# Layer 1's cross-attention as a pipeline of single tiles, three of them begun in the self-attention

## The chip, the cores and the metric

The kernel runs on one core of a Trainium2 chip. A core has a matrix engine (TensorE, PE in the profile, with its weight loads as PEld), three engines for elementwise work (VectorE or DVE, ScalarE or ACT, GpSimd or POOL), and queues that start transfers (SyncE, or SP). Every engine works through its own instructions in order, and engines wait for each other through semaphores. TensorE writes to PSUM, which holds eight banks of 128 x 512 floats; the other memory is SBUF.

The metric is the device time of one execution in microseconds. A lower number is better.

## The reference

Two decoder layers with a layernorm after each sub-layer work on `x` of shape (2, 1024, 256), so on 2048 tokens. The change lies in the second layer's cross-attention, and it reaches into the self-attention before it:

```python
def _L1_xattn_ref(q, k, v, mask, wq, wk, wv, wo):
    # q: x (2, 1024, 256); k and v: ctx_1024 (2, 64, 256); 16 heads of 16
    qh = (q @ wq.T).reshape(bs, sq, N_HEADS, D_K).transpose(0, 2, 1, 3)
    kh = (k @ wk.T).reshape(bs, sk, N_HEADS, D_K).transpose(0, 2, 1, 3)
    vh = (v @ wv.T).reshape(bs, sk, N_HEADS, D_K).transpose(0, 2, 1, 3)
    z = jnp.einsum('bhqd,bhkd->bhqk', qh, kh) / math.sqrt(D_K)
    z = jnp.where(mask[:, None, :, :], jnp.float32(-10000000000.0), z)
    z = jax.nn.softmax(z, axis=-1)
    z = jnp.einsum('bhqk,bhkd->bhqd', z, vh)
    z = z.transpose(0, 2, 1, 3).reshape(bs, sq, D_MODEL)
    return z @ wo.T

x = _layernorm(x + _L1_attn_ref(...))     # x + 16-head self-attention, 1024 x 1024 scores
x = _layernorm(x + _L1_xattn_ref(x, ctx_1024, ctx_1024, mask_BxSxS2_bk1, wq, wk, wv, wo))
x = _layernorm(x + _L1_ffn_ref(x, ...))   # quantised: needs the largest |x| of all tokens first
```

Each token has 16 heads x 64 keys = 1024 scores. The feed-forward network after it scales its input by the largest absolute value of the whole layernorm's output, so it cannot begin before the last tile has been normalised.

## The kernel before

The 2048 tokens are four groups of 512 (`g`), two for each batch element, and 16 tiles of 128 (`n`). The stages follow each other: layer 0's attention, cross-attention and experts (`l0_attn`, `l0_xattn`, `l0_ffn`), layer 1's self-attention (`l1_attn`, L1205), its cross-attention (`l1_xattn`, L1647) and its feed-forward network (`l1_ffn`). While the experts run, the generator `prepare` (L1518) makes ready what layer 1 will need, one step of it at each of the expert steps from the fifth on: here the masks, the transposed weights of the cross-attention, its keys (`lxkT`) and values (`vblk`), and the quantised weights of the last network.

Inside a `manual_schedule` the engines that it names issue in the order in which the program is written. The other engines' order is made by a planner.

The self-attention goes by units. A unit is one block of 128 keys for four heads and 512 queries; there are 16 steps of 8 units. In each unit `maxima` computes scores on TensorE and takes their maxima on VectorE nine units ahead (L1285, L1295), `products` computes the scores again, transposed (L1331), adds the shift (L1338) and takes the exponentials on ScalarE (L1348), and `mix` multiplies those of the unit before by the values (L1362). Every eighth unit `shifts` and `shifted` turn the maxima into the next step's shift (GpSimd L1307 to L1309, TensorE L1316). The table `extra` puts other work behind the unit's own: `taken` and `quotient` for the step before (L1382 to L1387), and after the last heads of a group `turned` (L1400), `residual` (L1410, GpSimd), `output` (L1418), `normed` and `onward` (L154). What is left for the last group after the last unit is in `self.ends`, which the cross-attention calls. The written order holds for TensorE, VectorE and ScalarE there; GpSimd's is the planner's.

In the cross-attention only TensorE's order is written. A tile passes through these steps:

- `queries(g)` for a group: 2 x 2 products of 512 columns (L1671), scaled by 0.25 on the way out.
- `softmax(n)`: GpSimd fills a tile with -1e10 (L1683); TensorE computes the 1024 scores in two products over 128 rows, against keys laid out block by block so that each head meets only its own 16 rows (`kblk`, L1686); VectorE copies the scores that are not masked over the fill (L1690) and takes each head's maximum (L1695); GpSimd subtracts it (L1696); ScalarE takes the exponential (L1697).
- `turn(n)`: 8 transposes (L1707), copied out of PSUM by ScalarE and VectorE.
- `mix(n)`: 8 products of 34 columns (L1722): two heads' values and for each head a column of ones, so that the sum of the weights comes along. VectorE inverts the sums and scales (L1727, L1729).
- `back(n)`: two transposes (L1739), copied by ScalarE.
- `output(n)`: the projection (L1753), the addition (L1756), and on VectorE for three tiles and then one the layernorm (L175 to L228) and the largest absolute value (L1766).

Each fp32 product of TensorE is recorded as two instructions. A tile's PSUM comes from three rings: `bank` (three banks), `wide` (two times two banks) and `acc` (one bank).

## Time and profile before

| what | us |
| --- | --- |
| time, median of 3 runs | 2329.27 (2327.75 to 2330.91) |
| the profiled execution's own time | 2326.49 |
| its span, first to last instruction | 2324.7 |
| TensorE busy in the span | 2253.7 (97%) |
| VectorE, ScalarE, GpSimd busy | 1650.6, 1117.5, 916.0 |
| last maxima of the self-attention (L1285) | 2091.9 |
| last instruction of the self-attention's last mix (L1362) begins | 2122.1 |
| cross-attention's scores (L1686) | from 2128.4 |
| the last largest absolute value (L1766) | ends 2243.0 |

A line of a group reads: line of the program, engine, operation, what is written and read, their shapes, how often; then busy time, mean ns of one, and the idle time of the engine just before it with what ended most of that. Lines of a timeline or of the chain begin with the start and the length. Busy times of TensorE overlap a little, since its instructions are pipelined; start-to-start distances are the safer measure.

### The profile page before, as it was taken

To read this page: it belongs to the slowest core of one execution; us is meant where nothing else is said; L and a number is where in the kernel's file an instruction comes from. 1 tells how busy PE (TensorE), PEld (TensorE's weight loads), DVE (VectorE), ACT (ScalarE), POOL (GpSimd) and SP (SyncE) were. 2 spreads that over 40 slices of the span, in tenths; PEclk is the share of its full clock that TensorE was granted. 3 is DMA by queue.
4 is the path that set the end of the run, shared out by engine and by line. 5 is a ranking of instruction groups with operands and counts; after the bars stand their busy time and mean duration, and the time that the engine had idled before them with its cause. 6 is when DMAs were issued, how large, how long until landed. Compare 5 with 4: busy or idle time off the path is not lost.

```text
span 2324.7 us, 37116 instructions
## 1 busy us (share of the span) xinstructions
PE 2253.7 (97%) x13964; PEld 1558.2 (67%) x13969; DVE 1650.6 (71%) x2836; ACT 1117.5 (48%) x1754; POOL 916.0 (39%) x791
## 2 busy tenths in 40 slices
PE   8999999999999999999999999999999999999986
PEld 3555545555546788999999999999744454554752
DVE  5888788998787356555556555456789687994778
ACT  4666566566564322333233333333157565665355
POOL 4676576677566444324334333333211101102420
PEclk9999999999999999999999999999999999999998
DMA  6777678577686120101001011000313121310001
GB/s 155 175 174 170 147 180 185 133 182 176 143 196 165 41 62 1 37 15 31 19 32 37 19 31 37 15 1 1 62 17 51 25 45 28 52 22 1 1 1 37
DMA packets 103831, 168.68 MB, mean 73 GB/s; under 512 B 47602, under 2 KB 65508, under 8 KB 103652
## 3 DMA queue, kind: packets, MB, share of 16 engines
q1 hardware_dynamic: 96804, 147.94, 27.9%
q10 hardware_dynamic: 6848, 18.36, 3.3%
q8 instruction: 111, 1.82, 0.3%
q14 instruction: 68, 0.56, 0.1%
HBM read 34.10 MB, written 2.10 MB: 16 GB/s over the span
## 4 chain that ended last, share of the span: by engine, by line
PE 87%; DVE 6%; ACT 3%; issue 2%; DMA 1%; SPq 1%; POOL 0%; ACTq 0%; DVEq 0%; POOLq 0%
PE unit L1025 17%; PE acc L1073 10%; PE wide L325 10%; PE acc L410 9%; PE bank L1073 7%; PE acc L1362 5%; PE bank L280 4%; PE bank L1285 4%; PE bank L428 2%; PE bank L744 2%; PE wide L1331 2%; PE wide L1338 2%; PE bank L304 2%; DVE most L1295 1%; PE bank L1194 1%
## 5 line engine op out<-in xcount | busy, mean ns | idle before, releaser
L340 DVE TENSOR_REDUCE nm<-wide 128x1 f32<-128x1024 f32 x256 | 300.7, 1214 | 58.2 <-PE wide L325 57.1
L1348 ACT ACTIVATE w<-wide 128x1024 f32<-128x1024 f32 x256 | 248.2, 1021 | 128.4 <-PE wide L1338 127.5
L1295 DVE TENSOR_REDUCE most<-bank 128x1 f32<-128x512 f32 x476 | 295.4, 681 | 16.1 <-PE bank L1285 15.5
L325 PE MATMUL wide<-k,q 64*128 64x512 f32 x1024 | 264.3, 624 | 9.3 <-ACT p L345 7.6
L356 POOL TENSOR_SCALAR p<-p,sums 128x1024 f32<-128x1024 f32 x128 | 143.4, 1121 | 249.2 <-DVE sums L353 249.2
L410 PE MATMUL acc<-turned,v 128*64 128x256 f32 x2048 | 235.1, 382 | 0.2 <-issue 0.2
L410 PEld LDWEIGHTS acc<-turned,v 128*64 128x64 f32 x2048 | 141.8, 137 | 111.5 <-issue 35.0
L1014 ACT ACTIVATE mhT<-mhT,cols 128x256 f32<-128x256 f32 (+1 forms) x256 | 143.4, 607 | 146.5 <-DVE mhT L1042 103.4
L345 ACT ACTIVATE p<-wide,nm 128x1024 f32<-128x1024 f32 x128 | 142.8, 1115 | 125.0 <-DVE nm L340 104.6
L923 POOL TENSOR_TENSOR hs<-hs,mhT 128x1024 f32<-128x1024 f32 x31 | 102.4, 3304 | 237.5 <-DVE hs L921 220.2
L1025 PE MATMUL unit<-xT,w 128*128 128x256 f32 x768 | 182.2, 379 | 0.0
L370 DVE STREAM_TRANSPOSE blocks<-p 128x1024 f32<-128x1024 f32 x128 | 158.0, 1234 | 25.3 <-DMA turned<-blocks 9.2
L1082 DVE SCALAR_TENSOR_TENSOR r<-acc,gates,r 128x128 f32<-128x128 f32 x256 | 77.7, 345 | 138.1 <-PE acc L1073 138.1
L325 PEld LDWEIGHTS wide<-k,q 64*128 64x128 f32 x1024 | 89.8, 186 | 126.2 <-issue 78.1
L370 DVE STREAM_TRANSPOSE blocks<-r 128x1024 f32<-128x1024 f32 x128 | 153.8, 1202 | 0.0
L1025 PEld LDWEIGHTS unit<-xT,w 128*128 128x128 f32 x768 | 140.9, 190 | 17.0 <-issue 0.5
L356 POOL TENSOR_SCALAR r<-r,sums 128x1024 f32<-128x1024 f32 x128 | 143.8, 1124 | 0.0
L345 ACT ACTIVATE r<-wide,nm 128x1024 f32<-128x1024 f32 x128 | 142.1, 1111 | 0.0
L1285 PE MATMUL bank<-kst,qst 64*128 64x512 f32 x476 | 133.1, 471 | 9.2 <-DVE most L1295 8.0
L1362 PE MATMUL acc<-w,v 128*32 128x512 f32 x1024 | 137.6, 606 | 1.1 <-ACT w L1348 1.1
L1285 PEld LDWEIGHTS bank<-kst,qst 64*128 64x128 f32 x476 | 66.8, 185 | 107.0 <-DVE most L1295 80.9
L393 POOL COPY turned<-blocks 32x1024 f32<-32x1024 f32 x128 | 131.9, 1031 | 4.0 <-DVE blocks L370 0.3
(351 smaller groups left out, 4373.7 us busy)
## 6 DMA issues: line engine op xcount, KB each, us to landing
turned<-blocks SPq DMA_DIRECT2D x636, 128.0 KB, 2.4
turned<-blocks ACTq DMA_DIRECT2D x132, 128.0 KB, 2.5
w<-in_L_ffn_W SPq DMA_DIRECT2D x16, 1024.0 KB, 5.5
q<-q SPq DMA_DIRECT2D x64, 128.0 KB, 2.4
k<-k SPq DMA_DIRECT2D x32, 128.0 KB, 2.3
qst<-qh SPq DMA_DIRECT2D x48, 64.0 KB
qst<-ql SPq DMA_DIRECT2D x48, 64.0 KB, 2.3
kst<-kh SPq DMA_DIRECT2D x48, 64.0 KB, 2.3
```

The costliest lines, as they stand in the source:

```text
L325: nc.tensor.matmul(sc[h][:, kb, :], lhsT=q[rows, qi, at : at + P], rhs=k[rows, ki, :], start=True, stop=True,)
L340: nc.vector.tensor_reduce(nm, sc, AX.XY, ALU.max, negate=True)
L345: nc.scalar.activation(p, sc.rearrange("p a c -> p (a c)"), AF.Exp, bias=nm, accum_out=sums[:, 0, h : h + 1],)
L356: nc.gpsimd.tensor_scalar(p, p, sums[:, 1, h : h + 1], 1.0, ALU.mult, ALU.mult)
L370: nc.vector.transpose(blocks[m][:, :, :, h, qt, :], p.rearrange("p (k r q) -> p r k q", r=4, q=32))
L410: nc.tensor.matmul(av[own[h], 0:256].rearrange("p (t i q) -> p i t q", t=2, i=4), lhsT=vals[u][:, kt, own[h]], rhs=p[:, h], start=kt == 0, ...
L1025: nc.tensor.matmul(v[:, m, :], lhsT=up[e][k][:, f : f + P], rhs=self.halves[g][k], start=k in (1, 2, 5) and m == 0, stop=True, skip_group_ ...
L1073: nc.tensor.matmul(ps[at][:, m * P : (m + 1) * P], lhsT=h[k][:, c, m * P : (m + 1) * P], rhs=down[e][k][:, c, :], start=k in (1, 2, 5) and ...
L1285: nc.tensor.matmul(sc[a], lhsT=stack[b, jp, "q"][rows, q0 : q0 + P], rhs=stack[b, jp, "k"][rows, kb * 512 : (kb + 1) * 512], start=True, s ...
L1295: nc.vector.tensor_reduce(most[n][:, kb, qt, h : h + 1], sc[a], AX.X, ALU.max, negate=True)
L1348: nc.scalar.activation(slot[:, k, :], ps[k].rearrange("p a q -> p (a q)"), AF.Exp, scale=0.25)
L1362: nc.tensor.matmul(mixed[n][o : o + 32, :], lhsT=vals[b][:, kt, 17 * h : 17 * h + 32], rhs=pT[:, a, :], start=kt == 0, stop=kt == 7, tile_ ...
```

## The change

The cross-attention becomes two functions. `l1_cross` defines the steps of a tile up to its normalised weights, and `l1_attn` calls them for the first three tiles among its last 12 units. `l1_xattn` runs the rest in units of one tile, with the order of all four computing engines written out. In unit `u` a tile's weights are turned (`u-3`), the scores of tile `u` are computed and copied, the exponentials of tile `u-1` follow, then its sums and weights; the output belongs to tile `u-5`; odd units normalise a pair of tiles and even ones mix a pair.

- Scores: the keys are used in two halves of 64 rows, and four fp32 products over 256 columns take the place of two over 512. The mask is a bf16 product that starts the accumulation: -1e30 where a key is masked (`masked`, `never`), in place of the fill and the predicated copy. ScalarE copies the 1024 scores to SBUF (VectorE for the first three tiles).
- The weights are divided by their sums before they are turned: a sum on VectorE, a reciprocal, a multiplication on GpSimd (for the last two tiles the addition and the multiplication are shared with VectorE).
- Mix: for two tiles at once and transposed, with 32 columns of values in each of the four column groups of TensorE. No transpose back is needed; the columns of ones are gone.
- Layernorm: in pairs; statistics in an even unit, with the small addition on GpSimd, scaling in the following odd unit on ScalarE (VectorE for the last pair).
- Self-attention: GpSimd's order is written out as well. The keys' layout moves to GpSimd, 44 units before the end. `normed(2)` and `onward(2)` move from the self-attention's last units into the cross-attention's units 3 and 4; `turned(3)` and the two `output(3)` come one unit later each.
- `prepare`: four new steps make `masked` with 16 bf16 transposes. Every later step comes four expert steps later.

```diff
@@ moments
-        nc.vector.tensor_scalar(ve[:, 0:n], mv[:, 0:n, 1], EPS, None, ALU.add)
+        (by or nc.vector).tensor_scalar(ve[:, 0:n], mv[:, 0:n, 1], EPS, None, ALU.add)
@@ l1_attn
+            self.l1_cross()
+            x = self.cross
+            at(last - 44, x["keys"])
+            for m in range(2):
+                at(last - 11 + m, x["queries"], 0, m)
+                at(last - 2 + m, x["queries"], 1, m)
+            for n in range(3):
+                for f in ("scores", "copied"):
+                    at(last - 8 + 2 * n, x[f], n)
+                for f in ("exponentials", "weights") if n < 2 else ():
+                    at(last - 5 + 2 * n, x[f], n)
...
                     for k, f in ((10, turned), (10, residual), (14, normed), (16, onward)):
-                        at(first + k, f, g)
+                        if k < 14 or g < 2:
+                            at(first + k, f, g)
...
-            engines = {mybir.EngineType.PE, mybir.EngineType.DVE, mybir.EngineType.Activation}
+            engines = {
+                mybir.EngineType.PE, mybir.EngineType.DVE, mybir.EngineType.Activation,
+                mybir.EngineType.Pool,
+            }
...
             self.ends = [
-                lambda: (turned(3), residual(3)), lambda: [output(3, i) for i in (0, 2)],
-                lambda: normed(3), lambda: onward(3),
+                lambda: (residual(3), normed(2)), lambda: (turned(3), onward(2)),
+                lambda: output(3, 0), lambda: output(3, 2), lambda: normed(3), lambda: onward(3),
             ]
@@ prepare
+        for n in range(0, T // P, 4):
+            both = tmp.tile([P, 4, 2, SK], BF16, tag="both", name="both")
+            nc.vector.tensor_copy(both, mask[:, n : n + 4, :].unsqueeze(2).to_broadcast([P, 4, 2, SK]))
+            ps = self.ps_t.tile([P, 1024], BF16, tag="t", name="bankb")
+            for i in range(4):
+                nc.tensor.transpose(
+                    ps[:, i * P : (i + 1) * P], both[:, i].rearrange("p a k -> p (a k)"), self.identb
+                )
+            self.evac(self.masked[:, n * P : (n + 4) * P], ps[:, 0 : 4 * P])
+            yield
@@ l1_cross (new)
+        def scores(n):
...
+            for r, a in zip(rows, range(2)):
+                nc.tensor.matmul(
+                    ps[a], lhsT=self.masked[r, n * P : (n + 1) * P],
+                    rhs=self.never[r].rearrange("p h k -> p (h k)"), start=True, stop=True,
+                    skip_group_check=True,
+                )
+            for m in range(2):
+                for r, a in zip(rows, range(2)):
+                    nc.tensor.matmul(
+                        ps[a][:, m * 256 : (m + 1) * 256], lhsT=qT[g][r, m, i * P : (i + 1) * P],
+                        rhs=self.kblk[r, g // 2, m, 4 * a : 4 * a + 4, :].rearrange("p h k -> p (h k)"),
+                        start=False, stop=True, skip_group_check=True,
+                    )
+        def scaled(n, by, op):
+            p = prob[n]
+            halves = [(nc.gpsimd, 0, H)]
+            if n >= NT - 2:
+                halves = [(nc.gpsimd, 0, H // 2), (nc.vector, H // 2, H)]
+            for e, lo, hi in halves:
+                e.tensor_tensor(
+                    p[:, lo:hi, :], p[:, lo:hi, :],
+                    by[:, lo:hi].unsqueeze(2).to_broadcast([P, hi - lo, SK]), op,
+                )
+        def copied(n):
...
+            if n < 3:
+                for a in range(2):
+                    nc.vector.tensor_copy(
+                        p[:, 8 * a : 8 * a + 8, :].rearrange("p h k -> p (h k)"), ps[a]
+                    )
+            else:
+                nc.scalar.copy(p, ps.rearrange("p a (h k) -> p (a h) k", k=SK))
+            nc.vector.tensor_reduce(nm, p, AX.X, ALU.max, negate=True)
+            scaled(n, nm, ALU.add)
+        def exponentials(n):
+            if n < NT:
+                nc.scalar.activation(prob[n], prob[n], AF.Exp)
+        def weights(n):
...
+            nc.vector.tensor_reduce(z, prob[n], AX.X, ALU.add)
+            rz = self.sm.tile([P, H], F32, tag="lxrz", name="lxrz")
+            nc.vector.reciprocal(rz, z)
+            scaled(n, rz, ALU.mult)
@@ l1_xattn
+            def mix(r):
...
+                        nc.tensor.matmul(
+                            ps[o, c, :], lhsT=self.vblk[:, r // 4, 4 * c + q].rearrange("p a i -> p (a i)"),
+                            rhs=turned[r][:, 4 * (q // 2) + 2 * c + q % 2, :], start=True, stop=True,
+                            tile_position=(0, 32 * q),
+                        )
...
+                self.evac(mixed[r], ps, by=nc.scalar)
...
+            def normed(r):
...
+                by = nc.vector if r == NT // 2 - 1 else nc.scalar
+                self.scaled(new[g], res[g], range(i, i + 2), *moments.pop(r), by)
+                nc.vector.tensor_reduce(
+                    self.xm[:, r : r + 1], new[g][:, i : i + 2, :], AX.XY, ALU.max,
+                    apply_absolute_value=True,
+                )
...
+            with self.tc.manual_schedule(engines=engines):
+                for u in range(3, NT + 6):
+                    turn(u - 3)
+                    x["scores"](u)
+                    x["copied"](u)
+                    x["exponentials"](u - 1)
+                    x["weights"](u - 1)
+                    output(u - 5)
+                    if u % 2:
+                        normed((u - 7) // 2)
+                        if u > 3:
+                            x["queries"]((u + 4) // 4, u // 2 % 2)
+                    else:
+                        mix((u - 4) // 2)
+                    if u < 9:
+                        self.ends[u - 3]()
```

## The prediction

> **What bounds the kernel now.** The change rewrites the stage after layer 1's self-attention, so I read first the busy times of the engines in that stage, window by window (length, then busy us and instructions of PE, PEld, DVE, ACT, POOL, then granted clock):
>
> ```profile
> 2125.00:2150.00 25.00, 23.54 (x93) 13.86 (x93) 16.91 (x28) 8.08 (x12) 9.54 (x7) 1.00 0.00 1
> 2150.00:2176.00 26.00, 25.01 (x148) 18.70 (x147) 18.17 (x32) 8.82 (x14) 12.00 (x9) 1.00 0.00 1
> 2176.00:2202.00 26.00, 25.39 (x144) 18.59 (x143) 20.24 (x40) 8.44 (x13) 12.28 (x11) 1.00 0.00 1
> 2202.00:2228.00 26.00, 25.32 (x163) 20.04 (x162) 21.61 (x48) 9.86 (x15) 12.49 (x10) 1.00 0.00 1
> 2228.00:2243.00 15.00, 9.74 (x66) 7.88 (x65) 11.10 (x36) 2.99 (x5) 2.63 (x8) 0.95 0.00 1
> ```
>
> TensorE bounds it (97% busy, full clock); ScalarE is two thirds idle and no DMA runs. Then the chain of waits, for what one tile of 128 tokens costs TensorE:
>
> ```profile
> 2190.51 0.22 PE bank L1739 x2
> 2190.73 1.71 PE acc L1722 x16
> 2192.44 3.51 PE bank L1671 x8
> 2195.95 1.72 PE wide L1686 x4
> 2197.67 0.87 PE bank L1707 x8
> 2198.54 0.87 PE bank L1753 x4
> ```
>
> Mix 1.71, scores 1.72, turning the weights 0.87, output 0.87, turning back 0.22, and a quarter of the queries (3.51 for four tiles) 0.86: 6.25 us a tile. The output of one group of four tiles to that of the next (2189.38 to 2215.59) is 26.2, so 6.55 a tile. The groups of the stage give the other engines' prices (the column after the count: busy us, mean ns):
>
> ```profile
> L1696 POOL TENSOR_TENSOR lxp<-lxp,lxnm 128x1024 f32<-128x1024 f32 x16 | 30.4, 1902 | 34.0 <-DVE lxnm L1695 34.0
> L1690 DVE COPY_PREDICATED lxp<-keep,wide 128x1024 f32<-128x1024 uint8 x16 | 20.8, 1302 | 10.0 <-PE wide L1686 10.0
> L1695 DVE TENSOR_REDUCE lxnm<-lxp 128x16 f32<-128x1024 f32 x16 | 19.3, 1209 | 0.0
> L1697 ACT ACTIVATE lxp<-lxp 128x1024 f32<-128x1024 f32 x16 | 16.9, 1058 | 21.8 <-POOL lxp L1696 21.8
> ```
>
> Two more rows carry steps below. The timeline at the end of the self-attention: a layernorm stands ahead of the last exponentials on ScalarE, and the last mix waits:
>
> ```profile
> 2117.69 2.07 ACT L224 ACTIVATE xg<-r,off,rstd 128x256 f32<-128x256 f32 x4
> 2119.66 1.92 ACT L1348 ACTIVATE w<-wide 128x1024 f32<-128x1024 f32 x2
> 2120.72 1.96 PE L1362 MATMUL acc<-w,v 128*32 128x512 f32 x8 [1.14 <-ACT w L1348]
> ```
>
> And the clock after a pause: TensorE stood still for 3.3 us before 1694.28, at the self-attention's start, and ran at 0.54 and 0.78 in the ten us from 1695 (last but two column of each line):
>
> ```profile
> 1690.00:1695.00 5.00, 1.59 (x10) 0.79 (x12) 3.25 (x6) 0.69 (x1) 1.83 (x4) 1.00 0.57 93
> 1695.00:1700.00 5.00, 4.61 (x20) 2.37 (x20) 4.34 (x7) 3.22 (x3) 0.00 (x0) 0.54 0.01 3
> 1700.00:1705.00 5.00, 5.00 (x36) 2.32 (x34) 2.94 (x5) 3.05 (x4) 0.00 (x0) 0.78 0.00 0
> ```
>
> **The change part by part.** Pitches below are start to start, read off the timelines.
>
> *What a tile costs TensorE after.* Scores: four 64-row products over 256 columns in pairs on the two row halves. Layer 0's 64-row scores (L325) take 1.92 from start to start for four over 512, so 0.86 here and 0.2 of start-up; with the mask's bf16 pair (0.23, from the pair pitch of L1331; 0.43 if the halves don't overlap) 1.3. Mix: 16 instructions of 256 columns in four column groups for two tiles; L1362 does 8 of 512 in 1.0, so 0.5 a tile, and turning back is gone. Turn 0.87, output 0.87, queries 0.86 stay: 4.4 a tile with 0.1 per switch. TensorE no longer bounds.
>
> *What bounds then.* By their orders, unit u puts on ScalarE two evacuations of turned weights (L74: pitch 0.49 each), the copy of the scores (1.02; nearest L1348, also 128x1024 out of PSUM; as two L74 copies of 0.58 it would be 1.16), the exponential (0.97), and in odd units the layernorm's two scalings (1.0). VectorE: maximum 1.13, sum 1.24 (both L1695), reciprocal 0.17, addition 0.33, in even units the statistics 1.06, in odd ones the offset 0.16 and a maximum 0.6. In an odd unit this is a ring: VectorE cannot give the offset before maximum, sum, reciprocal and addition (3.0), ScalarE waits for it behind its exponential, scales (1.0), evacuates twice (1.0), copies (1.0), and only then has VectorE its next maximum: 6.1 with hand-overs. An even unit is VectorE's sum, 4.0. So 10.1 for two tiles, 5.05 a tile; the predicated copy (1.30) and its fills on GpSimd are gone, the sum and the copy have taken their places. GpSimd has 2 x 1.9 a unit and 0.9 of powers in even ones: 8.5 of 10.1. Its new multiplication has no row of that size; L680 (128x256, 0.615) times four gives 2.46, and 9.6 still fits: nothing either way. ScalarE alone: 7.5 of 10.1. TensorE: 8.7.
>
> *The self-attention's end.* Queries for groups 0 and 1 and three tiles' scores move ahead of the last mix, onward(2) out. Before, 2093.3 to 2125.1 (after the last quotient) is 31.8. Added: 2 x 3.4 queries and 3 x 1.3 scores; taken out 1.1 (onward) and about 2.1 of stalls, since ScalarE no longer scales there and queries cover the exponentials; banks held by copies, about 1.0. VectorE has 15 us of copies, maxima, sums to do in 23 and no more self-attention maxima: hidden. Sum +8.5: it ends at 2133.6.
>
> *Units 3 to 8*, from copy to copy on ScalarE. First copy done 2137.1 (turn 1.0, scores 1.3, copy 1.0). To unit 4: 6.9 (ring of an odd unit, four scalings of group 2 instead of two). To 5: 5.5, TensorE: mix 1.05, turned(3) 1.05, onward(2) 1.05, turn, scores, copy. But mix(0) waits for turned weights behind those scalings: TensorE pauses from 2138.3 to 2143.0. By the clock row it then runs at half for about 7 us: +3.5. To 6: 6.9 and to 7: 6.2, TensorE with the outputs of group 3 (1.95 each). To 8: 9.1, the ring with queries' evacuation 0.55 and four scalings 2.1 in it. To unit 9's maximum: 4.7. Sum 42.8: 2179.9.
>
> *Units 9 to 15.* Three pairs of 10.1, 0.9 for the evacuation of queries in unit 11, 0.7 for VectorE's half of the last additions: 31.9. Maximum of tile 15 at 2211.8.
>
> *The tail.* VectorE and ScalarE go to and fro over the last two layernorms: maximum to the exponential's end 7.5, sum and weights 2.5, turn and VectorE's queue 4.7, mix and evacuation 1.75, to the last addition 3.75, statistics, power, scaling, maximum 3.45: 23.6 (before, from its last maximum at 2222.35: 20.6). End 2235.4 against 2243.0: 7.6 less.
>
> *The preparation in layer 0's experts.* 16 bf16 transposes on a TensorE that is 99.6% busy from 690 to 1660; L1605 has 36 in 3.0 us: +1.4 (bounds 0, in a gap, and 3, one exposed evacuation of 0.4 per group). The later steps of the preparation come four expert steps later, one whole expert: same phase of the weight loads on SP's queue; 0, at worst the 3. The keys' four products move to GpSimd (L930 to L924: 1.27 to 2.02 each) 84 units in, where it waits 22 us between shifts: 0. GpSimd's order is now written out; its shifts wait for VectorE as before: 0. The weights' tiles lie in the self-attention's own key and query parts, last read by its transfers some 20 units earlier, so no copy waits for memory: 0.
>
> Sum: -7.6 + 1.4 = -6.2. The profiled execution took 2326.49 for a span of 2324.7; it becomes 2320.3. The median shown, 2329.27, lies 2.8 above that execution, so I forecast 2323.
>
> **A rule against it.** The row says that ScalarE's copies out of PSUM cost 0.49 and 1.02. The Trainium skill's page "TensorEngine Tiling (Array Packing)", PSUM Bottleneck, warns that after tiling the copy out of PSUM may become the bottleneck. By the rule alone a tile would need 2.3 us on ScalarE and the stage would be far faster; the rows make the ring, not the copies, the bound. "TensorE: Matmul & The Clock Gate", Part 1, gives back the full clock after about 3.4 us of work; by that the pause would cost 1.7 instead of the 3.5 of the row, and the forecast would be 2321.
>
> **The rivals.**
> - *Each engine at its own pace*: no ring shows, units run at 4.4, and the clock holds. For it: no engine is full. Against: the written order. Seven units x 0.65, six earlier ones about 4, clock 3.5: 12 less, 2311.
> - *Hand-overs add up*: each unit 0.3 longer, as the real 6.55 stands to 6.25 now. Thirteen units: 2327, no difference.
> - *The row halves don't overlap* (both write PSUM at once): scores 2.4, TensorE 10.9 per pair of units, +0.4 a tile and 3.3 in the self-attention: +9, 2332. L325 speaks against it.
> - *Slower: the clock stays down.* With TensorE waiting, pauses of 2.6 and 2.9 us come in units 11 and 18, near the 3.3 that brought 0.54. At 0.5, TensorE's 4.35 a unit becomes 8.7 instead of 5.05: seven units +25, 2348. It decides against the change once the clock's mean in units 9 to 15 is under 0.73 (6.2 / 7 = 0.9 a unit: 4.35 / 5.95).
>
> **How the numbers follow.** A measurement tells 0.2%, 4.7 us: faster is under 2324.6, slower over 2333.9. The forecast has 0.46 (its own range 2318 to 2329, of it 0.34 faster and 0.12 same); own pace 0.20, faster; hand-overs 0.14 (0.03 faster, 0.11 same); no overlap 0.08 (half same, half slower); clock 0.12, slower. So 0.57, 0.27 and 0.16. The range 2308 to 2338 leaves out the deep half of the clock case and the best of own pace.
>
> **What would show it.** In the stage, ScalarE's scalings should wait for VectorE's offset 1.8 us in odd units, copies of scores come 10.1 apart by twos, TensorE is under 90% busy, and the clock drops once near 2143. The self-attention should end 8.5 later, the last maximum near 2237 counting the experts' 1.4. Wrong: scalings that don't wait; a clock under 1 throughout; GpSimd as the last to arrive; a longer expert stage.

## The result and the profile after

The changed kernel takes 2334.97 us (median of 20 runs, 2327.63 to 2338.54); the kernel before, beside it, 2328.58 (2324.55 to 2333.55). The ratio is 1.0027, with a 95% interval of 1.0019 to 1.0035: slower by 4 to 8 us, where 6.2 us less had been forecast. The profiled execution took 2331.46 for a span of 2329.7.

Cut at five landmarks, the two profiled executions differ as follows. The landmarks are the first product of layer 0's cross-attention with `xvw` (L731 in both), the end of the experts' last product (L1073), the start of the self-attention's third mix (L1362 before, L1364 after), the start of its last quotient (the reciprocal, L1386 and L1388), and the last reduction of the largest values (L1804, L1904).

| stretch | before | after | difference | forecast |
| --- | --- | --- | --- | --- |
| up to layer 0's cross-attention | 754.4 | 751.8 | -2.5 | 0 |
| from there to the experts' end | 912.2 | 918.2 | +5.9 | +1.4 |
| experts' end to the third mix | 40.7 | 45.7 | +5.0 | 0 |
| third mix to the last quotient | 417.9 | 426.2 | +8.3 | +8.5 |
| last quotient to the last reduction | 117.9 | 103.2 | -14.7 | -16.1 |
| the rest | 81.7 | 84.7 | +3.0 | 0 |
| span | 2324.7 | 2329.7 | +5.0 | -6.2 |

The stage that the change is about did nearly what the prediction said. The first row is within what executions differ by: in the ten kernels run further on the first landmark lies between 749.7 and 757.0. The last row goes with TensorE's clock: the granted clock is 0.50 for 40.3 us of that stretch, in one other kernel too (a_noearly, which takes 84.6 us as well), and for 23.2 to 30.6 us in the kernel before and the nine others, which take 81.1 to 82.0. Whether the change brings these 3 us in every execution is not shown, since one execution of each kernel was profiled. What is left are two places that the prediction had taken for harmless.

The stage's windows of the changed kernel, cut as those of before were (length, then busy us and instructions of PE, PEld, DVE, ACT, POOL, then granted clock):

```profile
2125.00:2150.00 25.00, 20.32 (x130) 9.85 (x122) 12.20 (x23) 14.07 (x19) 10.56 (x8) 1.00 0.00 1
2150.00:2176.00 26.00, 24.10 (x152) 16.34 (x152) 17.87 (x34) 15.43 (x23) 18.36 (x13) 0.93 0.00 1
2176.00:2202.00 26.00, 20.37 (x136) 12.71 (x136) 17.48 (x31) 17.90 (x29) 16.82 (x13) 1.00 0.00 1
2202.00:2228.00 26.00, 18.47 (x128) 11.51 (x132) 19.00 (x32) 17.20 (x27) 16.27 (x13) 0.89 0.00 1
2228.00:2243.00 15.00, 9.12 (x59) 5.23 (x50) 9.72 (x26) 5.96 (x10) 4.04 (x11) 0.95 0.00 0
```

TensorE is busy 78% and 71% of the third and fourth window, where it had 97%; no engine is full. The groups that answer those of before (the column after the count: busy us, mean ns):

```profile
L1748 POOL TENSOR_TENSOR lxp<-lxp,lxrz 128x1024 f32<-128x1024 f32 x6 | 11.4, 1904 | 0.0
L1769 ACT COPY lxp<-wide 128x1024 f32<-128x1024 f32 x7 | 7.1, 1013 | 2.3 <-PE wide L1736 2.3
L1770 DVE TENSOR_REDUCE lxnm<-lxp 128x16 f32<-128x1024 f32 x7 | 8.5, 1215 | 11.2 <-ACT lxp L1769 11.2
L1781 DVE TENSOR_REDUCE lxz<-lxp 128x16 f32<-128x1024 f32 x7 | 8.5, 1210 | 1.2 <-ACT lxp L1775 1.2
```

GpSimd's new multiplication costs the 1.90 of its addition, ScalarE's copy 1.01. The chain of waits through an even unit's end and the odd unit 11 shows what bounds now (start, length, what):

```profile
2197.20 1.17 DVE lxnm L1770
2198.37 1.14 DVE lxz L1781
...
2199.53 0.25 DVE lxrz L1783
2199.78 0.28 DVE r L1849
2200.06 1.10 DVE off L219
...
2201.18 1.09 ACT xg L224 x2
2202.27 0.49 ACT kl L76
...
2202.81 0.70 PE wide L1736 x4
```

Maximum, sum, reciprocal, addition and offset on VectorE follow each other, and only then can ScalarE scale, evacuate and let TensorE go on: the ring of the prediction. One of its links is longer than expected, the offset with 1.10 (1.17 as an instruction; the chain counts from the end of the instruction before).

At the end of the self-attention no layernorm stands on ScalarE any more, and the mix beside the last pair of exponentials but one does not wait (before, one waited 1.14 there); start, length, engine:

```profile
2131.55 1.06 ACT L1775 ACTIVATE ql<-ql 128x1024 f32<-128x1024 f32 x1
2132.39 1.07 PE L1364 MATMUL acc<-w,v 128*32 128x512 f32 x8
2132.50 1.94 ACT L1350 ACTIVATE w<-wide 128x1024 f32<-128x1024 f32 x2
```

**The first place: the experts.** TensorE's timeline has four entries that stop it; in brackets, the idle time ahead and what ended it:

```profile
988.17 0.40 PE L1562 MATMUL bankb<-identb,both 128*128 128x128 bf16 x4 [1.04 <-DVE both L1559]
...
1014.25 0.40 PE L1562 MATMUL bankb<-identb,both 128*128 128x128 bf16 x4 [1.04 <-DVE both L1559]
...
1040.33 0.40 PE L1562 MATMUL bankb<-identb,both 128*128 128x128 bf16 x4 [1.04 <-DVE both L1559]
...
1066.41 0.40 PE L1562 MATMUL bankb<-identb,both 128*128 128x128 bf16 x4 [1.04 <-DVE both L1559]
```

Each is the step that transposes four tiles of the mask. VectorE makes the copy `both` in the same step, so TensorE, which has the transposes next in its order, waits 1.04 us for it, on an engine that is otherwise full. Four times 1.04 is 4.2, and four times 0.40 of transposes 1.6: 5.8 us.

**The second place: the hand-over from the experts to the self-attention.** The queue on SP issues the transfers that stack keys (`kst`) and queries (`qst`) for the first maxima. Before, the first `qst` follows the first `kst` at once:

```profile
1655.36 3.23 SPq L1261 DMA_DIRECT2D kst<-xg  x4
1658.81 0.51 SPq L1261 DMA_DIRECT2D qst<-xg  x1
```

In the changed kernel it starts 9.5 us after the first `kst`:

```profile
1658.78 3.22 SPq L1263 DMA_DIRECT2D kst<-xg  x4
1668.24 0.51 SPq L1263 DMA_DIRECT2D qst<-xg  x1
```

The queue's waits of the changed kernel name what ended the gap (us in total, times, longest us): the last expert's products.

```profile
SPq L1263 <- PE acc L1073: 6.1, 1, 6.1
```

The transfer reads nothing that this product writes, so what ties them can only be the memory that it writes to. The self-attention's pools are put one on top of the other in the order in which they are opened. `qk` now has to outlive the self-attention, so it is opened first, and everything else moves up by its 34 KB and by the 4 KB of `lxq`. The addresses of the built programs (bytes in each partition) show where that puts the first two query stacks:

```
                      before              after
first qst             142816 - 146912     181984 - 186080
second qst            155104 - 159200     194272 - 198368
mhT, last expert      169568 - 185952     171104 - 187488
hs, last expert       191072 - 203360     192608 - 204896
```

Before, the first lay in the preparation's memory, and the second in the hidden tile `mhT` of the last expert but one (153184 to 169568). After, both lie in tiles that the last expert's products still read. TensorE then stands still and starts again at half clock (the list names `kst` as the last to come, though the first queries' transfers were being issued until 1670.9, on SP's queue and on ScalarE's):

```profile
1672.80 1.76 PE L1287 MATMUL wide<-kst,qst 64*128 64x512 f32 x4 [2.81 <-DMA kst<-xg]
1674.49 3.78 PE L1244 MATMUL bank<-w,xT 128*128 128x256 f32 x8
```

Eight products L1244 took 3.78 us here, and 1.99 at full clock before. In the windows, the last column but two is the granted clock:

```profile
1670.00:1675.00 5.00, 2.20 (x5) 1.18 (x6) 1.44 (x3) 0.00 (x0) 0.00 (x0) 0.80 0.86 196
1675.00:1680.00 5.00, 5.00 (x14) 3.14 (x13) 3.15 (x5) 0.00 (x0) 0.00 (x0) 0.52 0.76 139
```

Before, both windows have 1.00.

### The profile page after: what moved, and what is told of

Read it like the earlier page. It is cut to its first block, busy times and chain, and to the rows that moved or that the text cites. A ratio compares the mean times of both kernels' runs of the same rounds, so it can differ in the third digit from the quotient of the medians.

```text
span 2329.7 us, 37002 instructions
## 1 busy us (share of the span) xinstructions
PE 2237.6 (96%) x13916; PEld 1536.8 (66%) x13921; DVE 1643.6 (71%) x2803; ACT 1141.8 (49%) x1788; POOL 933.8 (40%) x800
## 4 chain that ended last, share of the span: by engine, by line
PE 86%; DVE 7%; ACT 3%; issue 1%; DMA 1%; SPq 1%; POOL 0%; ACTq 0%; DVEq 0%; POOLq 0%
PE unit L1025 16%; PE acc L1073 10%; PE wide L325 9%; PE acc L410 9%; PE bank L1073 7%; PE acc L1364 5%; PE bank L280 4%; PE bank L1287 4%; PE bank L428 2%; PE bank L744 2%; PE bank L304 2%; PE wide L1333 2%; PE wide L1340 2%; DVE most L1297 1%; PE bank L1194 1%
## 5 line engine op out<-in xcount | busy, mean ns | idle before, releaser
L1014 ACT ACTIVATE mhT<-mhT,cols 128x256 f32<-128x256 f32 (+1 forms) x256 | 143.4, 607 | 146.2 <-DVE mhT L1042 104.7
L1364 PE MATMUL acc<-w,v 128*32 128x512 f32 x1024 | 136.4, 605 | 0.0
```

The costliest lines, as they stand in the source:

```text
L1364: nc.tensor.matmul(mixed[n][o : o + 32, :], lhsT=vals[b][:, kt, 17 * h : 17 * h + 32], rhs=pT[:, a, :], start=kt == 0, stop=kt == 7, tile_ ...
```

## The experiments

Two theories stood against each other. The first: the pipeline gains as forecast, and the two places, each with a cause of its own, take more than the gain. The second: the stage itself gains too little, and the waits in the two places belong to each other or to the written order on GpSimd. All runs are timed against the kernel before on the same chip; its median was 2327.2 to 2327.7. b_order, b_mask, a_both and a_lag ran on one chip, a_ahead, a_right, a_port and a_best on a second, a_noearly and a_warm on a third.

**b_order: the kernel before, with the pools in another order.**

```diff
-            one, stp, qkp, rawp = pool("la1", 1), pool("st", 2), pool("qk", 1), pool("raw", 1)
+            qkp, one, stp, rawp = pool("qk", 1), pool("la1", 1), pool("st", 2), pool("raw", 1)
```

> The kernel before, with the one pool of the self-attention that holds its keys' and queries' parts opened ahead of the pool of their stacks instead of behind it, as in the changed kernel; nothing else differs. Theory (place): the first query stack then lies in memory that the last expert still reads, its transfer starts some 6 us later, TensorE stands still for about 2.8 us at the start of the self-attention and runs at half clock after it; the third mix of the self-attention comes about 5 us later and the time is about 5 us longer (2333.5 against 2328.5, +0.2%). Rival (order): the wait came with GpSimd's written order or with the later end of the experts, and not from the place; then nothing moves, within 1 us.

Measured: 2333.75 us, ratio 1.0026 (1.0015 to 1.0036). The third mix comes 44.4 us after the experts' end instead of 40.7. Its queue waits as in the changed kernel (SP's waits, and TensorE's):

```profile
SPq L1261 <- PE acc L1073: 5.9, 1, 5.9
```

```profile
PE wide L1285 <- DMA qst<-xT: 2.9, 1, 2.9
```

No instruction was added or moved between engines, and GpSimd's order is still the planner's. The place alone makes the wait; the rival is out. The half clock that was expected behind it did not come: after its pause of 2.87 us TensorE goes on at 1.00 (last column but two), so the hand-over costs 3.7 us here and not 5.

```profile
1670.00:1675.00 5.00, 2.15 (x9) 1.42 (x10) 2.11 (x6) 0.00 (x0) 0.28 (x1) 1.00 0.89 196
1675.00:1680.00 5.00, 4.94 (x23) 3.07 (x22) 5.00 (x9) 0.00 (x0) 0.00 (x0) 1.00 0.76 134
```

The other 2.8 of the 6.5 us by which the medians differ are not in this place; the interval of the ratio, 3.5 to 8.4 us, holds the 3.7.

**b_mask: the kernel before, with the mask steps alone.**

```diff
+        self.masked = late.tile([P, T], BF16, name="masked")
         yield
+        for n in range(0, T // P, 4):
+            both = tmp.tile([P, 4, 2, SK], BF16, tag="both", name="both")
+            nc.vector.tensor_copy(both, mask[:, n : n + 4, :].unsqueeze(2).to_broadcast([P, 4, 2, SK]))
+            ps = self.ps_t.tile([P, 1024], BF16, tag="t", name="bankb")
...
+            self.evac(self.masked[:, n * P : (n + 4) * P], ps[:, 0 : 4 * P])
+            yield
```

> The kernel before, with only the four mask steps of the preparation added (a copy on VectorE, four bf16 transposes, an evacuation, each), whose result nobody reads. Theory (copy ahead): in each step TensorE waits 1.04 us for the copy that VectorE starts in the same step, and works 0.4 us: 5.8 us longer experts (four waits of 1.0, 1.6 of transposes), 2334 against 2328.5, +0.25%. Rival (transposes alone, the prediction's step): 1.4 us, and the 1.0 us waits of the changed kernel belong to something else in it. The hand-over to the self-attention should be that of the kernel before in both.

Measured: 2334.05 us, ratio 1.0028 (1.0014 to 1.0042). From layer 0's cross-attention to the experts' end 918.2 us, to 0.1 that of the changed kernel; the hand-over is that of before (40.73). TensorE's waits:

```profile
PE bankb L1540 <- DVE both L1537: 4.1, 4, 1.0
```

**a_ahead and a_right: the changed kernel with one repair each; a_both: with both.** The first repair makes each copy at the end of the step before, in the same tile:

```diff
+        def twin(n):
+            if n < T // P:
+                twins[n] = tmp.tile([P, 4, 2, SK], BF16, tag="both", name="both")
+                nc.vector.tensor_copy(
+                    twins[n], mask[:, n : n + 4, :].unsqueeze(2).to_broadcast([P, 4, 2, SK])
+                )
+        twin(0)
         yield
         for n in range(0, T // P, 4):
-            both = tmp.tile([P, 4, 2, SK], BF16, tag="both", name="both")
-            nc.vector.tensor_copy(both, mask[:, n : n + 4, :].unsqueeze(2).to_broadcast([P, 4, 2, SK]))
+            both = twins.pop(n)
...
             self.evac(self.masked[:, n * P : (n + 4) * P], ps[:, 0 : 4 * P])
+            twin(n + 4)
             yield
```

The second puts the two pools that outlive the self-attention on the other side of SBUF, so that the stacks stay low (first `qst` at 143072):

```diff
-            qkp = self.l1qkp = self.hold.enter_context(self.pool("qk", 1))
-            self.lxq = self.hold.enter_context(self.pool("lxq", 1))
+            qkp = self.l1qkp = self.hold.enter_context(self.pool("qk", 1, side="right"))
+            self.lxq = self.hold.enter_context(self.pool("lxq", 1, side="right"))
```

> The changed kernel with only the first repair, the mask steps' copies a step ahead. Theory (two separate causes): the experts lose the four waits of 1.04 us and the hand-over to the self-attention keeps its 2.8 us wait: 4.1 us less than the changed kernel, about +0.1% on the kernel before. Rival (one cause brings the other: the experts' later end sets off the wait for the stacks): both go, and the time is that with both repairs, 0.15% under the kernel before.

> The changed kernel with only the second repair, the pools that outlive the self-attention on the other side of the memory. Theory (two separate causes): the 2.8 us wait at the hand-over and the slow clock behind it go, the experts stay 5.8 us longer than before: 5 us less than the changed kernel, about +0.05% on the kernel before. Rival (the new place brings waits of its own in the cross-attention's tiles): the stage after the self-attention gets longer than its 104.7 us.

> The changed kernel with both repairs: each mask step's copy is made at the end of the step before, and the pools that outlive the self-attention stand on the other side of the memory, so that the first stacks lie where they lay before. Theory (place and copy ahead): the four waits of 1.04 us and the wait of 2.8 us with its slow clock are gone: 4.1 + 5.0 = 9 us less than the changed kernel, about 2326, 2.5 us less than before (ratio 0.999). Rival (the stage itself costs more than it gains): the repairs give under 4 us and the time stays over 2331.

| kernel | us | ratio to before | experts | hand-over | last mix to last reduction |
| --- | --- | --- | --- | --- | --- |
| before | 2327.2 to 2328.6 | 1 | 912.2 | 40.7 | 120.3 |
| after | 2334.97 | 1.0027 (1.0019 to 1.0035) | 918.2 | 45.7 | 104.6 |
| a_ahead | 2327.09 | 0.9997 (0.9986 to 1.0008) | 913.3 | 46.0 | 104.6 |
| a_right | 2328.12 | 1.0007 (0.9998 to 1.0016) | 918.2 | 40.2 | 104.8 |
| a_both | 2323.52 | 0.9984 (0.9973 to 0.9994) | 913.3 | 41.9 | 104.7 |

(Experts: from the `xvw` product to the experts' end. Hand-over: from there to the third mix. The last column begins with the end of the self-attention's last mix.) Each repair takes away its own wait and leaves the other: a_ahead keeps the wait of 2.8 us for the stacks, a_right keeps the four waits. So the causes are separate, and the stage has no wait from its new place. The hand-over column also holds how long the half clock lasts after a pause of 3.3 us that every kernel has at the start of the self-attention: 3.4 us in a_right and 10.2 in a_both, which goes with the 1.7 by which these two differ without the wait. With both repairs the change is worth 0.06 to 0.27%: 3.7 us where 6.2 were forecast.

All three gained more than was expected: 7.9 us by the medians for a_ahead (4.1 expected), 6.9 for a_right (5.0) and 11.4 for a_both (9), where the two columns account for 4.5, 5.4 and 8.6. The three profiled executions have no long last stretch (81.6 to 81.7 us, 84.6 in the changed kernel); whether those 3 us are the rest is not shown.

**a_lag: with both repairs, and the scalings a unit on.** `normed` is cut in two: `offset` is its instruction on VectorE and stays in the odd unit; `late`, the two scalings on ScalarE and the maximum on VectorE, comes behind the mix of the next even unit (8 to 16).

```diff
                     if u % 2:
-                        normed((u - 7) // 2)
+                        (offset if u < 17 else normed)((u - 7) // 2)
...
                         mix((u - 4) // 2)
+                        if u < 18:
+                            late((u - 8) // 2)
```

> The changed kernel with both repairs, and in units 7 to 15 the layernorm's two scalings on ScalarE moved one unit on, behind that unit's mix, so that ScalarE no longer waits for VectorE's offset behind the sum of the weights; the offset stays where it is. Theory (ring): an odd unit loses the 2.3 to 3.1 us wait of ScalarE, the pair of units falls from 10.2 us to what GpSimd and TensorE need (8.7 to 9.2): five pairs, about 5 to 6 us less than with both repairs alone, about 2320. Rival (hand-overs): the wait was cover for another one, maximum or evacuations arrive just as late, and the time stays within 1.5 us of that with both repairs alone.

Measured: 2311.92 us, ratio 0.9935 (0.9921 to 0.9949), 11.6 less than a_both; the stage from the last mix takes 94.9 us instead of 104.7. ScalarE's timeline of the changed kernel at the odd unit 11, and of a_lag around the unit 10 that now holds the scalings of the pair before:

```profile
2197.01 1.06 ACT L1775 ACTIVATE lxp<-lxp 128x1024 f32<-128x1024 f32 x1
2201.18 1.09 ACT L224 ACTIVATE xg<-r,off,rstd 128x256 f32<-128x256 f32 x2 [3.11 <-DVE off L219]
```

```profile
2188.62 0.59 ACT L74 COPY lxo<-acc 128x512 f32<-128x512 f32 x1 [0.17 <-PE acc L1838]
2189.11 1.09 ACT L1882 ACTIVATE xg<-r,off,rstd 128x256 f32<-128x256 f32 x2
2190.10 1.06 ACT L74 COPY lxpT<-bank 128x512 f32<-128x512 f32 x2
```

The scalings of units 8 to 14 wait for nothing any more, those of unit 16 for 0.63 us. Copies of scores two units apart stand 9.4, 9.2 and 8.7 us apart (units 9 to 15) instead of 10.2, 11.7 and 10.2. That is 4.9 us in these three pairs of units, about what the theory said for all five; 1.5 more comes before unit 9 and 3.5 behind the copy of tile 15, which the expectation had left out: the layernorm of tiles 8 and 9 waited 5.25 us for its offset there. So the ring is confirmed, but its worth was put at half of what it is.

**a_port: with both repairs, and the offset with one tensor operand.** In the changed kernel the offset is one `scalar_tensor_tensor` on two small tensors in SBUF.

```diff
-            nc.vector.scalar_tensor_tensor(
-                off[:, 0:2], mv[:, 0:2, 0], -1.0, rstd[:, 0:2], ALU.mult, ALU.mult
-            )
+            for k in range(2):
+                nc.vector.tensor_scalar(
+                    off[:, k : k + 1], mv[:, k, 0:1], rstd[:, k : k + 1], -1.0, ALU.mult, ALU.mult
+                )
```

> The changed kernel with both repairs, the layernorm's offset in the pipeline computed by two instructions with one tensor operand each, the power as a scalar of its row, instead of one with two tensor operands in SBUF; order and place unchanged. In the changed kernel the offset of units 7 to 15 takes 0.39, 0.39, 1.17, 0.90 and 0.67 us where it takes 0.15 elsewhere, and ends within 0.04 us of the addition or multiplication that GpSimd is in. Theory (VectorE waits for GpSimd with two tensor operands): the offsets fall to 0.15 to 0.30 each, ScalarE's scalings come 0.2 to 0.9 us earlier in each odd unit, the stage is 1.5 to 2.5 us shorter than with both repairs (104.75 us). Rival (the offset waits for the power by its semaphore): the new instructions show the same lengths or idle time ahead of them, and nothing is gained.

Measured: 2319.43 us, ratio 0.9971 (0.9960 to 0.9983); the stage from the last mix 102.5 us, 2.3 less than a_both. (The intervals of the two ratios overlap, so the gain rests on the traces.) VectorE's offset of unit 11 in the changed kernel and GpSimd's addition beside it:

```profile
2199.97 1.17 DVE L219 SCALAR_TENSOR_TENSOR off<-mv,rstd 128x2 f32<-128x2 f32 x1
```

```profile
2199.23 1.90 POOL L1748 TENSOR_TENSOR lxp<-lxp,lxnm 128x1024 f32<-128x1024 f32 x1
```

They end at 2201.14 and 2201.13. In a_port the two instructions that take its place run through while GpSimd is at work:

```profile
2189.81 0.32 DVE L1871 TENSOR_SCALAR off<-mv,rstd 128x1 f32<-128x1 f32 x2
```

All pairs but one take 0.32 us (one 0.33). The rival, a wait for the power's semaphore, would have kept them late; but ScalarE's wait for the offset in units 9, 11 and 13 is now 2.14 us each time, where it was 2.33, 3.11 and 2.84.

**a_best: all of it, and group 2's scalings behind unit 4's mix.** Their offset stays in unit 3, the scalings and `turned(3)` come in unit 4, group 2's turning in unit 5; the copies for the values' block in the experts also come a step ahead.

```diff
-                lambda: (residual(3), normed(2)), lambda: (turned(3), onward(2)),
+                lambda: (residual(3), shifted2()), lambda: (scaled2(), turned(3)),
...
                     if u % 2:
...
+                        if u == 5:
+                            self.onward2()
```

> Both repairs, the scalings a unit on, the offset with one tensor operand; and besides the scalings of group 2 (four on ScalarE) moved from unit 3 to unit 4, behind the mix, with group 2's turning to unit 5; and the copies for the values' block a step ahead of their products in the experts. Theory: the pause of TensorE of 4.8 us in unit 4 falls to under 2.5 us and the clock does not drop there, 2 to 4 us less in units 3 to 9; the experts lose a wait of 1.1 us; the offset brings little here, as ScalarE no longer waits for it. In all 3 to 5 us less than with the lag alone (2311.9), ratio about 0.992. Rival: the queries of group 2 come later in unit 5 and hand the gain back; the time stays within 1.5 us of 2311.9.

Measured: 2308.52 us, ratio 0.9923 (0.9907 to 0.9938), 3.4 less than a_lag by the medians; the intervals of the two overlap, so that it is faster than a_lag is read from the traces. TensorE's first mix of the stage in the changed kernel and in a_best:

```profile
2150.83 2.40 PE L1828 MATMUL acc<-lxpT,vblk 128*32 128x256 f32 x16 [4.80 <-ACT lxpT L74]
```

```profile
2133.29 1.54 PE L1856 MATMUL acc<-lxpT,vblk 128*32 128x256 f32 x16 [0.34 <-ACT lxpT L74]
```

The pause of 4.80 us ahead of it, which a_lag still has, has become 0.34, and the clock stays at 1.00 from there to the end of the mixes. In the traces 2.5 us of the gain are in the stage (94.9 to 92.4) and 1.4 in the experts (913.3 to 911.9).

**a_noearly: with both repairs, and the pipeline begun after the self-attention.**

```diff
-            for n in range(3):
-                for f in ("scores", "copied"):
-                    at(last - 8 + 2 * n, x[f], n)
-                for f in ("exponentials", "weights") if n < 2 else ():
-                    at(last - 5 + 2 * n, x[f], n)
...
-                for u in range(3, NT + 6):
+                for u in range(NT + 6):
```

> The changed kernel with both repairs, but the three tiles' scores, copies, exponentials and weights are not begun in the self-attention: the pipeline starts with unit 0 instead of unit 3 after the last mix; keys and queries of groups 0 and 1 stay where they are. Theory (the early tiles hide the pipeline's filling): the self-attention is 3.6 us (three scores at 1.2) to 5.5 us (with the waits for banks) shorter than 424.7; the stage after it gets longer by the way of tile 0 alone through scores 1.2, copy 1.3, maximum 1.2, addition 1.9, exponential 1.0, sum 1.2, multiplication 1.9 and turning 1.0, about 10 us; net +5, about 2328. Rival (the early tiles cost in the self-attention what they save): both change by the same and the time stays within 1.5 us of that with both repairs (2323.5).

Measured: 2333.40 us, ratio 1.0021 (1.0011 to 1.0031), 9.9 more than a_both. The self-attention from the third to the last mix is 3.1 us shorter (424.7 to 421.6), the stage 13.7 longer. TensorE stands still for 4.8 us until tile 0 is through all engines, and goes on at half clock:

```profile
2140.37 1.97 PE L1815 MATMUL bank<-ident,qh 128*128 128x128 f32 x8 [4.82 <-POOL qh L1753]
```

Eight transposes take 1.97 us here, 1.04 elsewhere in this stage; the expectation of 10 us for the filling had left the clock out, which is at 0.50 for 6.8 us here and 3.4 us after a second pause. The early tiles are worth more than the 3.1 us that they cost the self-attention. What the other parts of the change (the mask as a product, the mix for two tiles, the scores in halves) are worth singly, no run separates.

**a_warm: as a_best, and 44 transposes of the identity, read by nobody, in the last pause.**

```diff
+                ps = self.bank()
+                for i in range(44):
+                    nc.tensor.transpose(ps[:, i % 4 * P : (i % 4 + 1) * P], self.ident, self.ident)
```

> The version with all repairs, and 44 transposes of the identity on TensorE (0.109 us each, 4.8 us, nobody reads them) in the pause of 5.8 us between the last output and the scale's transpose. Theory (the pause costs the clock of the FFN's start): TensorE starts the FFN at full clock instead of half for its first 8 us, the FFN (81.3 to 82.1 us from the scale's last reduction) is 2 to 3 us shorter. Rival (the FFN's start is bound by ScalarE and VectorE, or the pauses of 0.5 to 1.4 us after the transposes bring the half clock anyway): under 1 us.

Measured: 2306.31 us, ratio 0.9910 (0.9894 to 0.9925); the intervals of the two overlap. The last stretch takes 81.1 us against 81.2. The windows after the last output of a_warm, from its transposes into the feed-forward network:

```profile
2225.00:2230.00 5.00, 2.79 (x23) 2.31 (x21) 2.77 (x11) 0.43 (x2) 0.93 (x2) 1.00 0.00 0
2230.00:2235.00 5.00, 3.35 (x12) 1.96 (x14) 0.59 (x2) 4.66 (x7) 0.00 (x0) 0.62 0.00 0
2235.00:2240.00 5.00, 5.00 (x22) 2.72 (x21) 3.05 (x5) 3.50 (x6) 0.00 (x0) 0.69 0.00 0
```

The clock falls all the same, in the network's own pauses of 0.5 to 1.4 us between its first products. The rival holds, in its second form: the pauses bring the half clock anyway.

## Why the prediction was wrong

The forecast was -6.2 us, the measurement +6.4 (+5.0 in the profiled execution). The steps, by their names in the prediction:

- **The preparation in layer 0's experts, +1.4 with the bounds 0 and 3: this step failed.** The 16 transposes cost what was said: with the copies ahead, the experts of a_ahead are 1.1 us longer than before. But the step counted TensorE's instructions only. The copy that feeds them is in the same step, and TensorE waits for it four times. The upper bound took one exposed evacuation of 0.4 per group, behind the transposes; the exposed copy ahead of them was not priced, though the step of the diff shows it right above. Measured +5.9, of it 4.2 for the four waits.
- **"No copy waits for memory": this step failed.** It asked only for the tiles of the weights in the cross-attention, which lie in the key and query parts. The diff's first lines in `l1_attn` change the order in which the pools are opened, and with it the place of every stack. The first query stack then waits 6.1 us for the last expert's products, and TensorE 2.8. Measured +5.0 with the clock; between kernels that differ only in the place 3.7 (before and b_order), 4.1 (a_both and a_ahead) and 5.4 (a_right and after), by how long the half clock lasts.
- **The self-attention's end, +8.5: right.** Measured +8.3. Three scores cost 1.2 us each (2142.57 to 2143.75 in the stage), queries 2 x 3.4 and `onward` out as said. That the sum fits so well is partly luck: without the early tiles a_noearly is 3.1 us shorter here, where 3.9 for the scores and 1.0 for the banks had been added.
- **Units 3 to 8, 42.8 us: right in sum, 42.1.** From copy to copy 7.3, 7.1, 6.6, 6.0, 9.1, and 5.9 to unit 9's maximum, against 6.9, 9.0, 6.9, 6.2, 9.1, 4.7. Two terms are off and nearly cancel: the way to unit 9's maximum is 1.2 longer, and the pause in unit 4 came (4.80 us, 4.7 forecast), but the clock was back after 3.4 us, which costs 1.7 at most, not 3.5. The windows around it (granted clock in the last column but two):

```profile
2147.44:2150.85 3.41, 0.02 (x2) 0.02 (x2) 0.76 (x2) 2.61 (x6) 3.41 (x3) 1.00 0.00 0
2150.85:2154.26 3.41, 3.41 (x21) 1.87 (x22) 2.06 (x2) 2.86 (x4) 2.27 (x2) 0.50 0.00 0
2154.26:2157.67 3.41, 3.11 (x29) 2.61 (x29) 1.90 (x4) 2.21 (x4) 3.00 (x2) 1.00 0.00 0
```

  The Trainium skill ("TensorE: Matmul & The Clock Gate", Part 1), which gives back the full clock after about 3.4 us of work, was right here and the row that was taken was not; after the pause of 2.8 us at the hand-over TensorE was back at full clock only 6.8 us later (eight products L1244 from 1679.35 on take 2.20, the next eight 1.99), as the row said, so neither holds for every pause.
- **Units 9 to 15, 31.9: measured 33.3**; the copies by twos 10.2, 11.7 and 10.2 us apart, where 10.1, 11.0 and 10.1 were said. The scalings wait 2.3, 3.1 and 2.8 us for the offset in units 9, 11 and 13, not 1.8; most of the difference is the offset itself, 0.39, 1.17 and 0.90 instead of 0.16, and about 0.3 us of each is left in a_port too (2.14). a_lag shows that this ring bounds the units.
- **The tail, 23.6: measured 24.8.** The last layernorms go to and fro as said, but the clock falls a second time there, to 0.50 from 2222.5 to 2229.4, where the prediction had one fall in the stage.

Of the rivals, *no overlap* is out (scores 1.2, not 2.4), and so is *the clock stays down*: from 2154.3 to 2222.5, past the maximum of tile 15, the granted clock is 1.00. *Own pace* (2311) did not come, since the ring shows; a_lag (2311.9) and a_best (2308.5) reach that time, but with other orders of the program. *Hand-overs add up* is nearest to the stage, which is 1.4 us longer than forecast, where that rival had 3.9. GpSimd is no bound, as said: the multiplication of 1.90 fits. TensorE's turning waits for it in units 14 and 16 (0.94 and 2.03 us), but ScalarE, which has to copy the turned weights, waits longer for the offset just then (2.84 and 5.25). The chance of 0.16 for slower came from two rivals that did not happen. A longer expert stage stood only among the signs of being wrong, without a price above 3, and a wait for memory at the hand-over stood nowhere.

Together: +10.9 where +1.4 stood for the first two steps, and 1.4 in the stage (two terms in units 9 to 15 and the tail, 2.6, less 1.1 in the others). The first and the last row of the table add 0.5 to the profiled execution. The repaired kernel a_both shows the rest of the forecast: -3.7 us by the runs, where it had -6.2.

## What to carry to other kernels

A change is costed where it is issued, not where it is aimed: for each instruction put into another stage, look at what feeds it in that stage, because an engine with a written order and no idle time pays in full for a 1 us operand that starts in the same step. When a diff changes the order or the lifetime of memory pools, write down what the first tiles of the next stage land on and who reads that last. When a pipeline's bound is a ring of hand-overs between engines, moving the one link that another engine waits for (the scalings, one unit on) was worth 11.6 us, three times the net gain of the repaired change.

## What the runs showed that was not expected

VectorE's `scalar_tensor_tensor` on two SBUF tensors of two or four columns ends with the GpSimd instruction that runs beside it: 0.39 to 1.17 us instead of 0.15, in six units within 0.03 us of GpSimd's end, while reductions, reciprocals and additions out of PSUM keep their length. One operand given as the row's scalar takes the wait away. The Trainium skill states the rule ("SBUF — State Buffer", Who interferes with whom): a VectorE instruction with two SBUF inputs contends with a GpSimd instruction that reads SBUF, for a pair of ports that it calls an exclusive lock. These runs agree.

How long TensorE paused did not decide what its clock did. The pause of 2.35 us ahead of 2202.8 left the clock of the changed kernel at 1.00; the same pause, 2.34 us, brought it to 0.50 in a_noearly. The pause of 2.81 us at the changed kernel's hand-over brought it down, that of 2.87 in b_order did not. After the pause of 3.3 us at the start of the self-attention all twelve profiled executions ran at half clock, but two of them for 3.4 us, four for 6.8 and six for 10.2; in the kernels that do not wait there, the hand-over column is 40.2 with the first, 40.7 to 41.4 with the second and 41.9 to 42.5 with the third. In a_warm, 4.97 us of transposes that ended 1 us ahead of the next product did not hold the clock through the feed-forward network's start. A price for the clock taken from one pause is therefore good to a few us at best in this kernel.
